# An RWKV layer with a routed feed-forward: the first block's keys and values by seven products, the recurrence's differences clipped by Relu on ScalarE

## The chip, the cores and the metric

The kernel runs on one core of one Trainium2 chip. The core has five engines that run side by side, each in the order of its own queue: TensorE (matrix products; the profile has PE for the products and PEld for its weight loads), VectorE (DVE), ScalarE (ACT), GpSimd (POOL) and SyncE (SP), which here only issues transfers. The metric is device microseconds for one execution of the whole program, a median over runs.

## The reference, cut to what matters

```python
xn = layernorm(x)                                  # x: 1 x 2048 x 512
r, v, k = split(einsum('btc,dc->btd', xn, W_rvk))  # three 512 x 512 weights

def step(carry, kv):                               # over the 2048 tokens, per channel
    p, q, o = carry
    kt, vt = kv
    no = maximum(o, u + kt)
    A, Bc = exp(o - no), exp(u + kt - no)
    y = (A * p + Bc * vt) / (A * q + Bc)
    no2 = maximum(w + o, kt)
    A2, B2 = exp(w + o - no2), exp(kt - no2)
    return (A2 * p + B2 * vt, A2 * q + B2, no2), y

attn = einsum('btc,dc->btd', sigmoid(r) * wkv(k, v), W_out)
# feed-forward: softmax over 12 choices, the best 2 taken; 8 are experts (512 -> 256 -> 512,
# silu(gate) * up, then down), 4 pass xn through
out = x + attn + ffn(xn)
```

## The kernel before

**Tiling.** The 2048 tokens are taken as four blocks of 512 (`b`), the 512 channels as four columns of 128 partitions (`c`). `xnT[b]` holds a block of normalised tokens, transposed. `wrvk_sb[0]`, `[1]` and `[2]` are the weights of r, v and k.

**Products of a block.** k and v of one column together are, plainly, eight matrix products of half a block by half the channels. They can be had from seven, with sums of tokens (`S1` to `S4`, `sum_tokens`) and of weights (`T2` to `T4`, `sum_weights`; the first is made in place by `sum_first_weights`, L413). Each product is two matmuls of 256 tokens. `sevens(b, c, with_r)` gives the seven as steps `m1` to `m7`, `pair(b, c)` strings them together for two columns and their r (`A`, `B`, `R`). Product 5 multiplies `S1` by the weights that `sum_first_weights` makes. After products 2 and 3 an addition on VectorE is owed (`owe`): k gets the second product straight from PSUM, v gets `more`.

**Block 0** is different in the kernel before: k of columns 0 and 1 is multiplied plainly in halves by `half_k`, v and r of these two plainly by `project`, and columns 2 and 3 by `seven`, which makes k and v by seven products and r plainly.

**Order.** Everything up to the end of the planned part stands in an order written by hand (`manual_schedule`): each engine runs its instructions as the program lists them. `products` is a generator of steps, each of 0.86 us of TensorE, and `fill(n)` lists the next n steps. The head does, in this order: norms and transposes of the four blocks with one or two steps between them (7 steps), `sum_weights` and the four token sums of block 0, the routing's first part on VectorE, `fill(9)`, a small product `pc`, more routing with `sum_first_weights()` at L816, `fill(16)`, the products `pi` in two halves with `fill(2)` between them, then `which_i`, `emit(2)` (lists two owed additions), and the copy of `pi` and what follows from it (L955 to L968). Then the gathers and first fetches are issued, and L1280 to L1289 list the last steps of the head among owed additions, token sums of block 1 and sums of r's weights (`sum_r_weights`).

**PSUM.** All eight banks are taken: `ps_o`, `ps_mm`, `ps_gu` and `ps_tr` have two each. Behind the last step of block 0 `change_banks` (L91) closes the last three and opens `gu` (1), `p2` (1), `p1` (2), `p3` (1) and `pr` (1) in their place; in the order of opening, `gu` and `p2` take the banks of `ps_mm`, `p1` those of `ps_gu`, and `p3` and `pr` those of `ps_tr`. A pool that takes the banks of another may be written once every tile of the old pool has been read for the last time, wherever in the order that read is listed.

**The planned part.** From L1292 a table of due times orders the rest: 16 units of the recurrence (`scan(b, c)`, each in five stages), 23 tiles of the experts (`first_half`, `second_half`), the products of blocks 1 to 3, and the output products (`attention`). `UNIT` sets the distance of two units. In a unit VectorE makes the running maximum o2 (L351), a2 (L353) and b2 (L354); ScalarE takes their exponentials (L356, L357); VectorE runs two more scans (L363, L365), copies the state (L372, L373), forms numerator and denominator (L374 to L376) and divides (L380, L382).

**Loads.** SP issues x of block 0, the weight of k, the classifier, x of blocks 1 and 2, the weight of v, x of block 3, the weight of r (L124 to L132).

Of the kernel before, what the change touches and what calls it, by code (L numbers as in the profile page):

```python
# [26 lines left out]
F32 = mybir.dt.float32  # L27
# [8 lines left out]
P = 128  # L36
# [27 lines left out]
def layer(ctx: ExitStack, tc: tile.TileContext, x, w_rvk, w_out, decay, first, cls, ebias, gu, down, out):  # L64
# [60 lines left out]
    load_w(2)  # L125
# [3 lines left out]
    load_x(2)  # L129
    load_w(1)  # L130
    load_x(3)
    load_w(0)  # L132
# [132 lines left out]
    first_k = {}  # L265

    def half_k(c, h):
        if h == 0:
            first_k[c] = ps_mm.tile([P, TB], F32, tag="mm", name=f"pk0_{c}")
        hs = slice(h * HALF, (h + 1) * HALF)  # L270
        for k in range(CC):
            nc.tensor.matmul(
                first_k[c][:, hs],
                wrvk_sb[2][:, k, c * P : (c + 1) * P],
                xnT[0][:, k, hs],
                start=(k == 0),
                stop=(k == CC - 1),
                skip_group_check=True,
            )
        if h == 1:  # L280
            kvr[0, c, "k"] = kvp.tile([P, TB], F32, tag="k", name=f"k0_{c}")
            nc.scalar.copy(kvr[0, c, "k"], first_k[c])
# [30 lines left out]
    def project(b, c, parts=(("k", 2), ("v", 1), ("r", 0))):  # L313

        n = f"{b}_{c}"
        for name, m in parts:
            ps = ps_mm.tile([P, TB], F32, tag="mm", name=f"p{name}{n}")
            for k in range(CC):
                nc.tensor.matmul(  # L319
                    ps,  # L320
                    wrvk_sb[m][:, k, c * P : (c + 1) * P],
                    xnT[b][:, k, :],
                    start=(k == 0),
                    stop=(k == CC - 1),
                )
                if k < CC - 1:
                    yield
            t = (erp if name == "r" else kvp).tile([P, TB], F32, tag=name, name=f"{name}{n}")
            if name == "r":
                nc.scalar.activation(t, ps, AF.Exp, scale=-1.0)  # L330
            else:
                nc.scalar.copy(t, ps)
            kvr[b, c, name] = t
            yield

    def scan(b, c):
# [9 lines left out]
        obv = wk1.tile([P, 3, TB + 1], F32, tag="obv", name=f"obv{n}")  # L346
        nc.vector.tensor_copy(obv[:, :, 0:1], s[:, 0:3].unsqueeze(2))
        o, bs, bvs = (obv[:, m, 0:TB] for m in range(3))
        o2, b2, bv = (obv[:, m, 1 : TB + 1] for m in range(3))
# [3 lines left out]
        nc.vector.scalar_tensor_tensor(a2, o, w, o2, ALU.add, ALU.subtract)  # L353
        nc.vector.tensor_sub(b2, k, o2)  # L354
        yield
        nc.scalar.activation(a2, a2, AF.Exp)  # L356
        nc.scalar.activation(b2, b2, AF.Exp)  # L357
# [3 lines left out]
        sums = wk1.tile([P, 2, TB], F32, tag="sums", name=f"sums{n}")  # L361
        sq, sp = sums[:, 0, :], sums[:, 1, :]
        nc.vector.tensor_tensor_scan(sq, bs, a2, s[:, 3:4], ALU.add, ALU.mult)  # L363
        nc.vector.tensor_mul(bv, b2, v)
# [3 lines left out]
        if b > 0:  # L368
            nc.scalar.activation(er, er, AF.Exp, scale=-1.0)
        num = yT[b][:, c, :]  # L370
        if b + 1 < NTB:
            nc.vector.tensor_copy(s[:, 0:3].unsqueeze(2), obv[:, :, TB : TB + 1])  # L372
            nc.vector.tensor_copy(s[:, 3:5].unsqueeze(2), sums[:, :, TB - 1 : TB])  # L373
        nc.vector.scalar_tensor_tensor(sq, b2, cf, sq, ALU.mult, ALU.add)  # L374
        nc.vector.scalar_tensor_tensor(er, er, 1.0, sq, ALU.add, ALU.mult)
# [48 lines left out]
    def sum_r_weights(first):  # L424
        if first:
            for n in (2, 3, 4):
                rsum[n] = sump.tile([P, 2, 2, P], F32, tag=f"R{n}", name=f"R{n}")
# [48 lines left out]
    def seven(b, c):  # L476

        n = f"{b}_{c}"
        cs = slice(c * P, (c + 1) * P)

        def bank(pool_, tag, name):
            return pool_.tile([P, TB], F32, tag=tag, name=f"{name}{n}")

        def place(pool_, name):
            kvr[b, c, name] = pool_.tile([P, TB], F32, tag=name, name=f"{name}{n}")
            return kvr[b, c, name]

        def multiply(ps, m, begin, end):
            a, w = factors(b, m)
            for k in range(2):  # L490
                nc.tensor.matmul(  # L491
                    ps[:, :HALF],
                    w[:, k, cs],
                    a[:, k, :],
                    start=(begin and k == 0),
                    stop=(end and k == 1),
                    skip_group_check=True,
                )

        def add(dst, src):  # L500
            nc.vector.tensor_add(dst, dst, src)

        def r_step(k):
            nc.tensor.matmul(  # L504
                pr, wrvk_sb[0][:, k, cs], xnT[b][:, k, :], start=(k == 0), stop=(k == CC - 1)
            )

        def next_sums(ns):
            if c == CC - 1 and b + 1 < NTB:
                for m in ns:  # L510
                    owe(lambda m=m: sum_tokens(b + 1, m))

        p1 = bank(ps_mm, "mm", "p1_")
        multiply(p1, 1, True, False)
        k = place(kvp, "k")
        nc.scalar.copy(k[:, :HALF], p1[:, :HALF])
        yield
        emit_owed()
        pr = bank(ps_tr, "tr", "pr")
        r_step(0)  # L520
        yield
        r_step(1)
        yield
        multiply(p1, 6, False, False)
        v = place(kvp, "v")
        nc.scalar.copy(v[:, :HALF], p1[:, :HALF])
        yield
        p3 = bank(ps_mm, "mm", "p3_")
        multiply(p3, 5, True, False)
        more = five.tile([P, TB], F32, tag="more", name=f"more{n}")  # L530
        nc.scalar.copy(more[:, HALF:], p3[:, :HALF])
        yield
        p2 = bank(ps_gu, "gu", "p2_")
        multiply(p2, 2, True, True)
        owe(lambda: add(k[:, :HALF], p2[:, :HALF]))
        next_sums((1, 2))
        yield
        multiply(p1, 7, False, False)
        nc.scalar.copy(v[:, HALF:], p1[:, :HALF])
        next_sums((3,))  # L540
        yield
        r_step(2)
        emit_owed()
        yield
        r_step(3)
        r = place(erp, "r")
        nc.scalar.activation(r, pr, AF.Exp, scale=-1.0)
        yield
        multiply(p1, 4, False, True)
        nc.scalar.copy(k[:, HALF:], p1[:, :HALF])  # L550
        yield
        multiply(p3, 3, False, True)
        nc.scalar.copy(more[:, :HALF], p3[:, :HALF])
        owe(lambda: add(v, more))
# [3 lines left out]
    def sevens(b, c, with_r):  # L560
# [8 lines left out]
        def at(m):  # L569
# [8 lines left out]
            if m in (1, 2, 5):  # L578
                ps[which] = bank(which, f"{which}{'r' if with_r else ''}_{n}")
# [22 lines left out]
        def next_sums(*ns):  # L602
            if c == CC - 1 and b + 1 < NTB:
                for m in ns:
                    owe(lambda m=m: sum_tokens(b + 1, m))
# [11 lines left out]
        def m5():  # L617
            src = multiply(5)
            t["more"] = five.tile([P, TB], F32, tag="more", name=f"more{'r' if with_r else ''}{n}")
            nc.scalar.copy(t["more"][:, HALF:], src)  # L620
# [18 lines left out]
        return {1: m1, 2: m2, 3: m3, 4: m4, 5: m5, 6: m6, 7: m7}, next_sums  # L639

# [20 lines left out]
    def owe(work):  # L661
        owed.append((clock[0] + 2, work))
# [7 lines left out]
    LEAD = 2  # L670
# [623 lines left out]
    STEPS = 2 * 2 * CC + 11 * (CC - LEAD) + 21 * (len(units) - CC) // 2  # L1294
# [116 lines left out]
```

## Time and profile before

| | |
|---|---|
| median of 3 runs | 362.3 us (361.89 to 362.86) |
| the profiled execution's own time | 362.48 us |
| its span, first to last instruction | 360.7 us |
| TensorE busy | 98% of the span |
| VectorE busy | 85% |
| ScalarE busy | 44% |
| VectorE in units of the recurrence, longest group (reciprocal, L380) | 53.7 us |
| chain that ended last | PE 73%, DVE 17%, DMA 5% |

The times lie 1.8 us above the span. A busy TensorE is not a TensorE at its peak, since the ends of matmuls are modelled: whether it is dense is read from the starts of its rows. A matmul in fp32 is recorded as two instructions, so a step of two 256-token matmuls is "x4". In a timeline a row gives the start, the duration, the engine, the line and the operation, the tiles written and read, and in brackets the idle time before it.

### The profile page before, as it was taken

To read this page: it belongs to the slowest core of one execution; us is meant where nothing else is said; L and a number is where in the kernel's file an instruction comes from. 1 tells how busy PE (TensorE), PEld (TensorE's weight loads), DVE (VectorE), ACT (ScalarE), POOL (GpSimd) and SP (SyncE) were. 2 spreads that over 40 slices of the span, in tenths; PEclk is the share of its full clock that TensorE was granted. 3 is DMA by queue.
4 is the path that set the end of the run, shared out by engine and by line. 5 is a ranking of instruction groups with operands and counts; after the bars stand their busy time and mean duration, and the time that the engine had idled before them with its cause. 6 is when DMAs were issued, how large, how long until landed. Compare 5 with 4: busy or idle time off the path is not lost.

```text
span 360.7 us, 5328 instructions
## 1 busy us (share of the span) xinstructions
PE 354.0 (98%) x1850; PEld 256.7 (71%) x1850; DVE 306.8 (85%) x531; ACT 159.0 (44%) x308; POOL 90.3 (25%) x118
## 2 busy tenths in 40 slices
PE   8999999999999999999999999999999999999996
PEld 3764578799865877547877688988776988854344
DVE  5879889959999997899695799997989589979971
ACT  3576222354643645525545454546453546432000
POOL 6000300431312232321321433323322124221130
PEclk9999999999999999999999999999999999999999
DMA  8999950795869699967999968979979986924782
GB/s 282 398 356 363 331 174 2 245 323 135 254 196 248 147 367 301 276 215 189 281 281 334 294 189 216 309 147 306 284 226 262 236 173 167 337 55 58 177 139 95
DMA packets 47132, 84.46 MB, mean 234 GB/s; under 512 B 26496, under 2 KB 26880, under 8 KB 43328
## 3 DMA queue, kind: packets, MB, share of 16 engines
q1 hardware_dynamic: 39792, 64.05, 56.2%
q0 software_dynamic: 7312, 20.06, 25.1%
q8 instruction: 15, 0.25, 0.3%
q14 instruction: 13, 0.11, 0.1%
HBM read 63.25 MB, written 19.27 MB: 229 GB/s over the span
## 4 chain that ended last, share of the span: by engine, by line
PE 73%; DVE 17%; DMA 5%; ACT 2%; issue 1%; SPq 0%; DVEq 0%; ACTq 0%
PE pg L1109 19%; PE p L592 17%; PE po L1057 8%; PE pr L592 7%; PE pw L1244 7%; DVE r L380 4%; PE p L491 3%; DMA x<-in_x_dram 3%; DMA wrvk<-in_w_rvk_dram 2%; PE pr L504 2%; PE pr L319 2%; DVE sums L365 2%; DVE sums L363 2%; PE p2r L592 1%; PE po L1061 1%
## 5 line engine op out<-in xcount | busy, mean ns | idle before, releaser
L1109 PEld LDWEIGHTS pg<-xgT,gw 128*128 128x128 f32 x672 | 78.1, 192 | 3.7 <-ACT xgT L1090 1.6
L1109 PE MATMUL pg<-xgT,gw 128*128 128x128 f32 x672 | 79.1, 275 | 0.2 <-ACT xgT L1090 0.2
L1145 POOL DMA_INDIRECT out_dram<-yo,to_i x23 | 40.4, 1758 | 142.9 <-ACT yo L1141 28.7
L1244 PE MATMUL pw<-wout_sb,yT 128*128 128x512 f32 x120 | 54.1, 593 | 0.7 <-DVE xrows L1256 0.6
L380 DVE RECIPROCAL r<-r 128x256 f32<-128x256 f32 x32 | 53.7, 1719 | 0.0
L1244 PEld LDWEIGHTS pw<-wout_sb,yT 128*128 128x128 f32 x120 | 22.3, 190 | 25.5 <-issue 24.8
L1057 PE MATMUL po<-dw,act 128*128 128x512 f32 x84 | 39.5, 592 | 0.0
L1015 POOL DMA_INDIRECT xg<-xs,token_i x23 | 26.4, 1148 | 44.6 <-DVE empty L963 25.2
L1121 ACT ACTIVATE act<-pg 128x256 f32<-128x256 f32 x23 | 8.8, 384 | 65.0 <-PE pg L1109 60.4
L1122 DVE SCALAR_TENSOR_TENSOR act<-act,pg 128x256 f32<-128x256 f32 x23 | 9.6, 417 | 21.0 <-ACT act L1121 21.0
L1090 ACT COPY xgT<-xq 128x1024 uint16<-128x1024 uint16 x22 | 25.6, 1161 | 2.6 <-DMA xq<-xp 2.6
L1057 PEld LDWEIGHTS po<-dw,act 128*128 128x128 f32 x84 | 16.0, 190 | 13.7 <-issue 12.7
L592 PE MATMUL p<-xnT,wrvk 128*128 128x256 f32 x96 | 24.7, 380 | 0.7 <-DVE k L624 0.7
L592 PE MATMUL p<-S,wrvk 128*128 128x256 f32 x96 | 24.7, 380 | 0.0
L592 PE MATMUL p<-S,T 128*128 128x256 f32 x96 | 24.6, 379 | 0.0
L363 DVE TENSOR_TENSOR_SCAN sums<-obv,state,a 128x512 f32<-128x512 f32 x16 | 20.5, 1280 | 4.1 <-ACT obv L357 4.0
L1082 ACT COPY xp<-xg 128x1024 uint16<-128x1024 uint16 x22 | 23.0, 1047 | 0.0
L592 PEld LDWEIGHTS p<-xnT,wrvk 128*128 128x128 f32 x96 | 18.0, 190 | 6.0 <-issue 2.6
L592 PEld LDWEIGHTS p<-S,T 128*128 128x128 f32 x96 | 18.2, 190 | 5.0 <-issue 2.9
L365 DVE TENSOR_TENSOR_SCAN sums<-obv,state,a 128x512 f32<-128x512 f32 x16 | 20.6, 1288 | 0.6
L592 PEld LDWEIGHTS p<-S,wrvk 128*128 128x128 f32 x96 | 17.9, 190 | 4.3 <-issue 1.4
L351 DVE TENSOR_TENSOR_SCAN obv<-wdec,state,k 128x512 f32<-128x512 f32 x16 | 20.4, 1277 | 0.0
(262 smaller groups left out, 576.1 us busy)
## 6 DMA issues: line engine op xcount, KB each, us to landing
gw<-in_gu_dram SPq DMA_DIRECT2D x25, 1024.0 KB, 7.4
dw<-in_down_dram SPq DMA_DIRECT2D x25, 512.0 KB, 4.9
x<-in_x_dram SPq DMA_DIRECT2D x16, 256.0 KB, 6.4
xs<-x SPq DMA_DIRECT2D x16, 256.0 KB, 4.6
wrvk<-in_w_rvk_dram SPq DMA_DIRECT2D x3, 1024.0 KB, 7.2
xrow<-xs SPq DMA_DIRECT2D x8, 256.0 KB, 7.3
out_dram<-xrow POOLq DMA_DIRECT2D x8, 256.0 KB, 8.2
xrows<-xs SPq DMA_DIRECT2D x8, 256.0 KB, 6.4
```

The costliest lines, as they stand in the source:

```text
L351: nc.vector.tensor_tensor_scan(o2, w.to_broadcast([P, TB]), k, s[:, 0:1], ALU.add, ALU.max)
L363: nc.vector.tensor_tensor_scan(sq, bs, a2, s[:, 3:4], ALU.add, ALU.mult)
L365: nc.vector.tensor_tensor_scan(sp, bvs, a2, s[:, 4:5], ALU.add, ALU.mult)
L380: nc.vector.reciprocal(er[:, hs], er[:, hs])
L592: nc.tensor.matmul(dst, rows_(k), a[:, k, :], start=(first and k == 0), stop=(k == 1), skip_group_check=True,)
L1015: nc.gpsimd.indirect_dma_start(out=xg, out_offset=None, in_=xs, in_offset=bass.IndirectOffsetOnAxis(ap=token[:, column(i) : column(i) + 1] ...
L1057: nc.tensor.matmul(out_, lhs[:, c, :], rhs[0][:, c, :], start=(c == 0), stop=(c == last))
L1082: nc.scalar.copy(xp, st[i]["xg"].bitcast(U16).rearrange("p (c h) -> p h c", h=2))
L1090: nc.scalar.copy(xgT.bitcast(U16).rearrange("p c (t h) -> p c t h", h=2), st[i]["xq"].rearrange("p (h c) t -> p c t h", h=2),)
L1109: nc.tensor.matmul(pg[:, c // IC, c % IC * P : (c % IC + 1) * P], w[0][:, k, rs], xgT[:, k, :], start=(k == 0), stop=(k == CC - 1),)
L1145: nc.gpsimd.indirect_dma_start(out=out, out_offset=bass.IndirectOffsetOnAxis(ap=index, axis=0), in_=yo[ps], in_offset=None, compute_op=ALU ...
L1244: nc.tensor.matmul(po, yT[b][:, c, j * P : (j + 1) * P], wout_sb[:, c, :], start=(c == 0), stop=(c == CC - 1),)
```

## The change

In block 0, `half_k` becomes `half_r`: r of columns 0 and 1 is multiplied plainly in halves, and r of columns 2 and 3 plainly by `project_r`. k and v of all four columns come from the seven products, as steps of a new generator `first_pair`, for columns 0 and 1 and then for 2 and 3, each with an order written out. `seven` and `project` go. r of block 0 is now copied from PSUM, and its exponential is taken in the unit, as in the other blocks. The weights are loaded in the order r, k, v: r's in the place of k's, the other two behind all of x. The head lists one step fewer before the token sums and one more behind them, and the sums and owed additions in another order.

In a unit, VectorE forms only d = o + w - k; ScalarE makes relu(d) and relu(-d) and takes the exponentials of their negatives. The two sums are kept in the same tile as o2, b2 and bv, the denominator goes to `a2`, and the state is copied by one instruction of ScalarE. `UNIT` goes from 16.75 to 16.5, and four places of `after` move by one.

```diff
     load_x(0)
-    load_w(2)
+    load_w(0)
...
     load_x(1)
     load_x(2)
+    load_x(3)
+    load_w(2)
     load_w(1)
-    load_x(3)
-    load_w(0)
...
-        nc.vector.scalar_tensor_tensor(a2, o, w, o2, ALU.add, ALU.subtract)
-        nc.vector.tensor_sub(b2, k, o2)
+        nc.vector.scalar_tensor_tensor(a2, o, w, k, ALU.add, ALU.subtract)
         yield
-        nc.scalar.activation(a2, a2, AF.Exp)
-        nc.scalar.activation(b2, b2, AF.Exp)
+
+        nc.scalar.activation(b2, a2, AF.Relu)
+        nc.scalar.activation(a2, a2, AF.Relu, scale=-1.0)
+        nc.scalar.activation(b2, b2, AF.Exp, scale=-1.0)
+        nc.scalar.activation(a2, a2, AF.Exp, scale=-1.0)
         yield
...
+        nc.vector.tensor_mul(bv, b2, v)
         nc.vector.tensor_tensor_scan(sq, bs, a2, s[:, 3:4], ALU.add, ALU.mult)
-        nc.vector.tensor_mul(bv, b2, v)
         nc.vector.tensor_tensor_scan(sp, bvs, a2, s[:, 4:5], ALU.add, ALU.mult)
...
-        if b > 0:
-            nc.scalar.activation(er, er, AF.Exp, scale=-1.0)
+        nc.scalar.activation(er, er, AF.Exp, scale=-1.0)
         num = yT[b][:, c, :]
-        if b + 1 < NTB:
-            nc.vector.tensor_copy(s[:, 0:3].unsqueeze(2), obv[:, :, TB : TB + 1])
-            nc.vector.tensor_copy(s[:, 3:5].unsqueeze(2), sums[:, :, TB - 1 : TB])
...
+        if b + 1 < NTB:
+            nc.scalar.copy(s.unsqueeze(2), obv[:, :, TB : TB + 1])
...
+    def first_pair(c, order):
+        A, _ = sevens(0, c, False)
+        B, _ = sevens(0, c + 1, False)
+        for name in order.split():
+            {"A": A, "B": B}[name[0]][int(name[1])]()
+            yield
...
     def all_products():
-        for name, m in (("v", 1), ("r", 0)):
-            for u in range(LEAD):
-                yield from project(*units[u], ((name, m),))
-        for u in range(LEAD, CC):
-            yield from seven(*units[u])
+        for c in (2, 3):
+            yield from project_r(0, c)
+        yield from first_pair(0, "A1 B1 A2 A6 B6 B2 A7 B7 A5 B5 A4 B4 A3 B3")
+        yield from first_pair(2, "A1 B1 A5 A6 B6 B5 A7 B7 A3 A4 B4 B3 A2 B2")
         change_banks()
...
-    fill(4)
-    emit(3)
+    fill(3)
+    sum_tokens(1, 1)
+    emit(1)
+    sum_tokens(1, 2)
+    emit(1)
     sum_r_weights(True)
-    emit(1)
-    emit(1, 1)
+    sum_tokens(1, 3)
+    emit(2)
+    sum_tokens(1, 4)
     sum_r_weights(False)
-    emit(1)
+    emit(2)
     mixed_tiles()
     head = False
-    fill(8)
+    fill(9)
...
-    UNIT = 16.75
-    after = {10: (0, 0), 12: (0, 1), 16: (0, 2), 18: (0, 3), 27: (1, 0), 29: (1, 1), 36: (1, 2), 37: (1, 3)}
+    UNIT = 16.5
+    after = {10: (0, 0), 12: (0, 1), 16: (0, 2), 18: (0, 3), 26: (1, 0), 28: (1, 1), 35: (1, 2), 36: (1, 3)}
```

More of the change, by code (lines that the diff above doesn't have):

```diff
@@ L262, in turn_block, with half_r @@
             nc.scalar.copy(xnT[b][:, c, cols], pt[:, cols])
-    first_k = {}
-    def half_k(c, h):
+    first_r = {}
+    def half_r(c, h):
         if h == 0:
-            first_k[c] = ps_mm.tile([P, TB], F32, tag="mm", name=f"pk0_{c}")
+            first_r[c] = ps_mm.tile([P, TB], F32, tag="mm", name=f"pr0_{c}")
         hs = slice(h * HALF, (h + 1) * HALF)
@@ L272, in half_k @@
             nc.tensor.matmul(
-                first_k[c][:, hs],
-                wrvk_sb[2][:, k, c * P : (c + 1) * P],
+                first_r[c][:, hs],
+                wrvk_sb[0][:, k, c * P : (c + 1) * P],
                 xnT[0][:, k, hs],
@@ L280, in half_k @@
         if h == 1:
-            kvr[0, c, "k"] = kvp.tile([P, TB], F32, tag="k", name=f"k0_{c}")
-            nc.scalar.copy(kvr[0, c, "k"], first_k[c])
+            kvr[0, c, "r"] = erp.tile([P, TB], F32, tag="r", name=f"r0_{c}")
+            nc.scalar.copy(kvr[0, c, "r"], first_r[c])
     lgs = {}
@@ L311, in layer, with project_r @@
     yT, kvr = {}, {}
-    def project(b, c, parts=(("k", 2), ("v", 1), ("r", 0))):
+    def project_r(b, c):
         n = f"{b}_{c}"
[L316 to L334, printed above, removed]
+        ps = ps_mm.tile([P, TB], F32, tag="mm", name=f"pr{n}")
+        for k in range(CC):
+            nc.tensor.matmul(
+                ps,
+                wrvk_sb[0][:, k, c * P : (c + 1) * P],
+                xnT[b][:, k, :],
+                start=(k == 0),
+                stop=(k == CC - 1),
+            )
+            if k < CC - 1:
+                yield
+        kvr[b, c, "r"] = erp.tile([P, TB], F32, tag="r", name=f"r{n}")
+        nc.scalar.copy(kvr[b, c, "r"], ps)
+        yield
     def scan(b, c):
@@ L343, in scan @@
             yT[b] = xyp.tile([P, CC, TB], F32, tag="xy", name=f"yT{b}")
-        obv = wk1.tile([P, 3, TB + 1], F32, tag="obv", name=f"obv{n}")
-        nc.vector.tensor_copy(obv[:, :, 0:1], s[:, 0:3].unsqueeze(2))
+        obv = wk1.tile([P, 5, TB + 1], F32, tag="obv", name=f"obv{n}")
+        nc.vector.tensor_copy(obv[:, :, 0:1], s.unsqueeze(2))
         o, bs, bvs = (obv[:, m, 0:TB] for m in range(3))
-        o2, b2, bv = (obv[:, m, 1 : TB + 1] for m in range(3))
+        o2, b2, bv, sq, sp = (obv[:, m, 1 : TB + 1] for m in range(5))
@@ L358, in scan @@
+        nc.scalar.activation(a2, a2, AF.Relu, scale=-1.0)
+        nc.scalar.activation(b2, b2, AF.Exp, scale=-1.0)
+        nc.scalar.activation(a2, a2, AF.Exp, scale=-1.0)
         yield
         v = kvr[b, c, "v"]
-        sums = wk1.tile([P, 2, TB], F32, tag="sums", name=f"sums{n}")
-        sq, sp = sums[:, 0, :], sums[:, 1, :]
+        nc.vector.tensor_mul(bv, b2, v)
         nc.vector.tensor_tensor_scan(sq, bs, a2, s[:, 3:4], ALU.add, ALU.mult)
-        nc.vector.tensor_mul(bv, b2, v)
         nc.vector.tensor_tensor_scan(sp, bvs, a2, s[:, 4:5], ALU.add, ALU.mult)
@@ L367, in scan @@
         er = kvr[b, c, "r"]
-        if b > 0:
-            nc.scalar.activation(er, er, AF.Exp, scale=-1.0)
+        nc.scalar.activation(er, er, AF.Exp, scale=-1.0)
         num = yT[b][:, c, :]
-        if b + 1 < NTB:
-            nc.vector.tensor_copy(s[:, 0:3].unsqueeze(2), obv[:, :, TB : TB + 1])
-            nc.vector.tensor_copy(s[:, 3:5].unsqueeze(2), sums[:, :, TB - 1 : TB])
-        nc.vector.scalar_tensor_tensor(sq, b2, cf, sq, ALU.mult, ALU.add)
-        nc.vector.scalar_tensor_tensor(er, er, 1.0, sq, ALU.add, ALU.mult)
+        nc.vector.scalar_tensor_tensor(a2, b2, cf, sq, ALU.mult, ALU.add)
@@ L376, in scan @@
+        nc.vector.scalar_tensor_tensor(er, er, 1.0, a2, ALU.add, ALU.mult)
         nc.vector.scalar_tensor_tensor(num, bv, cf, sp, ALU.mult, ALU.add)
         yield
+        if b + 1 < NTB:
+            nc.scalar.copy(s.unsqueeze(2), obv[:, :, TB : TB + 1])
         def divide(h):
@@ L424, in sum_r_weights, with new @@
     def sum_r_weights(first):
+        def new(n):
+            t = sump.tile([P, TB], F32, tag=f"R{n}", name=f"R{n}")
+            rsum[n] = t.rearrange("p (k q n) -> p k q n", k=2, q=2)
         if first:
-            for n in (2, 3, 4):
-                rsum[n] = sump.tile([P, 2, 2, P], F32, tag=f"R{n}", name=f"R{n}")
+            new(3)
             rsum[1] = r_weights(0, 1)
@@ L431, in sum_r_weights @@
         else:
+            new(2)
+            new(4)
             nc.vector.tensor_add(rsum[2], rsum[3], r_weights(0, 0))
@@ L474, in r_factors @@
         return factors(b, n)[0], w
[L476 to L556, printed above, removed]
@@ L577, in at @@
                 return ps["pr"][:, h * HALF : (h + 1) * HALF]
-            if m in (1, 2, 5):
+            if m in (1, 2, 5) and not banks:
+                pool_, tag = {"p1": (ps_mm, "mm"), "p2": (ps_gu, "gu"), "p3": (ps_tr, "tr")}[which]
+                ps[which] = pool_.tile([P, TB], F32, tag=tag, name=f"{which}_{n}")
+            elif m in (1, 2, 5):
                 ps[which] = bank(which, f"{which}{'r' if with_r else ''}_{n}")
@@ L602, in next_sums @@
         def next_sums(*ns):
-            if c == CC - 1 and b + 1 < NTB:
+            if c == CC - 1 and 0 < b < NTB - 1:
                 for m in ns:
@@ L618, in m5 @@
             src = multiply(5)
-            t["more"] = five.tile([P, TB], F32, tag="more", name=f"more{'r' if with_r else ''}{n}")
+            if (b, c) in ((0, 2), (0, 3)):
+                t["more"] = sump.tile([P, TB], F32, tag=f"R{2 * c - 2}", name=f"more{n}")
+            else:
+                t["more"] = five.tile([P, TB], F32, tag="more", name=f"more{'r' if with_r else ''}{n}")
             nc.scalar.copy(t["more"][:, HALF:], src)
@@ L639, in sevens @@
         return {1: m1, 2: m2, 3: m3, 4: m4, 5: m5, 6: m6, 7: m7}, next_sums
+    def first_pair(c, order):
[3 more added lines that the diff above has]
+            {"A": A, "B": B}[name[0]][int(name[1])]()
+            yield
     def pair(b, c):
@@ L669, in layer @@
     units = [(b, c) for b in range(NTB) for c in range(CC)]
-    LEAD = 2
     def whole(gen):
@@ L709, in layer @@
     norm(0, late_js)
-    half_k(0, 0)
-    half_k(1, 0)
+    half_r(0, 0)
+    half_r(1, 0)
     turn_block(0, late_js)
@@ L720, in layer @@
         if b == 0:
-            half_k(0, 1)
+            half_r(0, 1)
         else:
@@ L725, in layer @@
         if b == 0:
-            half_k(1, 1)
+            half_r(1, 1)
         fill(1)
@@ L1293, in layer @@
     DONE = 7 + 9 + 16 + 2 + 12
-    STEPS = 2 * 2 * CC + 11 * (CC - LEAD) + 21 * (len(units) - CC) // 2
-    UNIT = 16.75
-    after = {10: (0, 0), 12: (0, 1), 16: (0, 2), 18: (0, 3), 27: (1, 0), 29: (1, 1), 36: (1, 2), 37: (1, 3)}
+    STEPS = 2 * CC + 7 * CC + 21 * (len(units) - CC) // 2
+    UNIT = 16.5
+    after = {10: (0, 0), 12: (0, 1), 16: (0, 2), 18: (0, 3), 26: (1, 0), 28: (1, 1), 35: (1, 2), 36: (1, 3)}
     groups = -(-(STEPS - DONE) // CC) + len(after)
```

## The prediction

> **What bounds the kernel now.** I read the busy shares first, then who TensorE waited for, then the starts of its rows.
>
> ```profile
> PE 354.0 (98%) x1850; PEld 256.7 (71%) x1850; DVE 306.8 (85%) x531; ACT 159.0 (44%) x308; POOL 90.3 (25%) x118
> PE warm L703 <- DVE ones L148: 1.1, 1, 1.1
> PE p L592 <- DVE k L624: 0.7, 1, 0.7
> PE pw L1244 <- DVE xrows L1256: 0.6, 1, 0.6
> PE pt L261 <- ACT x L247: 0.3, 1, 0.3
> PE pg L1109 <- ACT xgT L1090: 0.2, 1, 0.2
> ```
>
> From its first matmul on TensorE waits for another engine only 1.8 us in all (0.7 + 0.6 + 0.3 + 0.2). A busy share alone would not prove that it sets the pace, so I went through its timeline: from 8 us to 356 us a step of two matmuls starts 0.86 us after the one before and a tile's 16 up-products take 3.57 us, everywhere. Also behind 318 us, where the chain of waits runs through VectorE, the output products stand back to back from 324.0 to 340.5 (38 records in 16.5 us). So there is hardly a hole in which lost TensorE time could be won back: a wait of TensorE is worth its length, and so is a step less. The stage that decides is the head, where the change lists products and VectorE work in another order:
>
> ```profile
> 37.03 7.03 PE L319 MATMUL pr<-xnT,wrvk 128*128 128x512 f32 x16
> 43.90 0.22 PE L781 MATMUL pc<-hotb,ones 128*128 128x136 bf16 x1
> ...
> 44.58 1.08 PE L491 MATMUL p<-xnT,wrvk 128*128 128x256 f32 x4
> 45.49 1.88 PE L504 MATMUL pr<-xnT,wrvk 128*128 128x512 f32 x4
> 47.20 1.03 PE L491 MATMUL p<-S,T 128*128 128x256 f32 x4
> 48.07 1.03 PE L491 MATMUL p<-S,wrvk 128*128 128x256 f32 x4
> ...
> 61.59 1.59 PE L933 MATMUL pi<-tok,lowhot 128*128 128x200 bf16 x16
> ```
>
> ```profile
> 46.61 1.22 DVE L416 TENSOR_TENSOR wrvk<-wrvk,wrvk 128x1024 f32<-128x1024 f32 x1
> ...
> 64.29 0.36 DVE L955 COPY pis<-pi 128x200 f32<-128x200 f32 x1
> ...
> 65.76 0.41 DVE L501 TENSOR_TENSOR k<-k,p 128x256 f32<-128x256 f32 x1
> 66.09 0.68 DVE L445 TENSOR_TENSOR S<-xnT 128x512 f32<-128x512 f32 x1
> ...
> 71.28 0.68 DVE L501 TENSOR_TENSOR v<-v,more 128x512 f32<-128x512 f32 x1
> ```
>
> The first fence is TensorE's order, the second VectorE's at the same time. Product 5 (`p<-S,wrvk`) starts at 48.07, right behind L416, which makes its weights and ends at 47.83: between `pc` and it stand four steps that do not need them. And the k addition at 65.76 is VectorE's first work behind the copies of `pi`, ahead of the sums.
>
> **The products: -1.7 us.** Before, block 0 has 38 steps behind `half_k` (16 of `project`, 22 of `seven`), after it 36 (8 and 28), and `half_r` is as long as `half_k`. Two steps at 0.86 us (from 47.20 to 48.07 is one) are 1.7 us.
>
> **First wait: +3.3 us.** The head lists 7, 9, 16 and 2 steps as before. After the change the first 8 are r and the next 8, up to `pc`, are A1 B1 A2 A6 B6 B2 A7 B7 of the first pair. Step 17, the first behind `pc`, is A5, product 5. TensorE reaches it at 44.58, and nothing in the change moves `sum_first_weights`: L416 still ends at 47.83. Queued behind A5 is all of TensorE. It starts near 47.9, 3.3 us late. Both halves of `pi` are late next, and with them L955 on VectorE.
>
> **Second wait: +8.2 us.** The first three of the last steps are A2 and B2 of the second pair and then, as step 37, A1 of block 1. Between them `change_banks` puts `p1` on the banks of `ps_gu`, where A2 and B2 have just left their products. These are read by the owed additions to k of columns 2 and 3, and the owed list runs k, k, v, v, v, v, k, k: `emit(2)` behind the tiles takes the first two, and the last two stand at the very end of the new order. So A1 waits for VectorE's whole sequence. Call TensorE's end of `pi` zero. VectorE needs 0.2 to see it, 1.47 from L955 to the first work behind it (64.29 to 65.76), and then, from start to start in the rows of 65.76 to 71.88 (0.60 to 0.61 for 512 columns, 0.72 where the next one needs the result, 0.33 for a k addition): ten at about 0.60, two at 0.72, 0.33 and 0.41, together 8.2. The additions end at 9.9. TensorE is at A1 after A2 and B2, at 1.7: it waits 8.2 us. Next late is `turn(0)`, at 73.39 before, by both waits. The gathers and fetches (to landing 6.8 and 7.4 us) are issued off VectorE's copies, before these sums, and get 8 us more to land, so they add nothing.
>
> **The clock: +2.6 us.** No row of the head shows TensorE after such a pause. Nearest are two: after the 0.7 us wait at 101.85 the next steps come at the full rate, so the lower end is 0. At the start, after idling, the warm-up's loads come slowly first:
>
> ```profile
> 6.16 0.15 PEld L703 LDWEIGHTS <-ones 128*128 128x128 bf16 x1 [0.28 <-issue]
> 6.50 1.18 PEld L703 LDWEIGHTS <-ones 128*128 128x128 bf16 x6 [0.18 <-issue]
> ```
>
> From 1.06 to about 6.4 us they stand 0.43 apart, one to a row, then 0.21 (six in 1.18): half the rate for 5.3 us, which is 2.6 us lost, although the granted clock reads 1.00 in all of it. A pause of 8.2 us is nearer to the start's than to 0.7 us, so I take 2.6 for it, nothing for the one of 3.3, and 5.3 (both) for the upper end.
>
> [...]
>
> **The recurrence: +0.3 us.** VectorE loses L354 (0.60 us from start to start, 16 times) and the two state copies (0.32, 12 times): 13.4 us, against four more additions in block 0 (1.9 us). It is not the bound, so this buys at most the waits of TensorE for it, 0.7 at 101.85 and 0.6 at 342.5. ScalarE gains 32 relus, 12 copies and 4 exponentials. Relu is in no row: it can't cost less than nothing, and the nearest rows, L356 and L357, have 0.63 and 0.62 us (0.53 to 0.60 from start to start); I take 0.60. The copy is nearest to L947 with 0.2 us. Together 24 us on an engine with 202 us idle. What it delays are the operations queued behind the four in a row, 1.2 us each time. Where an `xgT` copy (L1090) follows soon and TensorE waits for it, that shows: at 161.55, where 0.2 us are lost already, and at 300.98, where 1.0 is spare. That is 1.2 + 0.2. At the other units 1.0 to 4.7 us are spare. VectorE's scans wait for the exponentials 4.0 us in all; the next one then has 1.2 us less lead and 0.6 less work before it, some 0.6 us in each of five units. The last unit's product stands 0.6 us later for it, about as much as TensorE waits there now. With 1.4 lost and 1.1 of the old waits won, I take +0.3, with -1.5 and +3 as ends.
>
> [...]
>
> **Loads: 0.** The last of the three weights has landed by 21.4 us (issued at 13.26, 8.1 us in the chain), and VectorE first adds weights at 29.9. These 8.5 us hide the new order; all of them are queued on SP within the same 13.6 us, with nothing new behind. If the cover were gone, VectorE would stall at L409.
>
> **The sum.** 362.5 (profiled execution) - 1.7 + 3.3 + 8.2 + 2.6 + 0.3 = 375.2. That execution lies 0.2 above the median, so **375.0 us**.
>
> **Rivals.**
> - *The banks do not hold A1.* If `p1` came to lie elsewhere, or the additions were earlier, the second wait and the clock go: 375.0 - 8.2 - 2.6 = 364.2. For it: no row before shows such a wait. Against: eight banks are full, and before the k addition is listed first. 8 in 100.
> - *Product 5 is not late*, since the change does not do what its order says and L416 comes earlier. Then L955 starts at 64.0, VectorE-bound, A1 is ready at 64.75 (63.02, the end of `pi`, and two steps) and waits for 73.7: 362.3 - 1.7 + 8.9 + 2.6 + 0.3 = 372.4. Against: L816 is not touched. 5 in 100.
> - *VectorE has set the pace all along*, and TensorE makes up what it loses. For it: 17% of the chain and nines in VectorE's slices. Then 13.4 - 1.9 = 11.5 us less work would cover the two waits' 11.5 us, the two steps and the two waits on VectorE go, 362.3 - 1.7 - 1.3 = 359.3. It decides from the point where TensorE has over 11.5 us of holes behind 76 us. Its rows have under 2. 5 in 100.
> - *More is lost behind ScalarE's queue* than I saw, or both waits go cold: 378 to 381. 6 in 100.
>
> **How the numbers follow.** The first forecast has 76 in 100. With both ends of the clock (0, 5.3) and the recurrence (-1.5, +3) it runs from 370.6 to 380.4; both at their ends together is unlikely, so I keep **370.5 to 378.5**, which also holds the second rival, about 8 in 10. A kernel like this can be told from no change beyond 0.3%, 1.1 us. Faster has the third rival and a little of the first, 0.06; the same 0.02; slower 0.92.
>
> **What would show it.** Right: TensorE idle some 3.3 us at 44.6, before the first product on `S` and `wrvk`, waiting for the VectorE operation of L416; idle some 8 us before the first product of block 1, waiting for an addition to k; weight loads at double spacing behind that; the middle dense, shifted by 10 to 13 us. Wrong: A1 following B2 at once, or holes in TensorE's middle that shrink by as much as the head loses.

## The result, and the profile after

| | before | after |
|---|---|---|
| median | 362.35 us (6 runs, 361.89 to 364.14) | 378.24 us (6 runs, 375.75 to 381.22) |
| ratio to before, 95% interval | | 1.043 (1.038 to 1.049) |
| profiled execution's own time, its span | 362.48, 360.7 us | 378.54, 376.8 us |
| granted TensorE clock, mean of the span | 1.000 | 0.982 |

The change makes the kernel 15.9 us slower. The forecast was 375.0 us, with 370.5 to 378.5 as its range: the median lies 0.3 us inside its upper end, and three of the six runs lie above it.

The page of the kernel after, its row of busy shares and its row of granted clocks over 40 slices (9 is full):

```profile
PE 357.8 (95%) x1874; PEld 264.1 (70%) x1874; DVE 296.6 (79%) x495; ACT 181.6 (48%) x364; POOL 89.9 (24%) x118
PEclk9999989859999999999999999999999999999999
```

Who TensorE waited for, in the same kernel (total us, times, longest):

```profile
PE p L512 <- DVE k L547: 8.1, 1, 8.1
PE p L512 <- DVE wrvk L410: 2.8, 1, 2.8
...
PE pw L1172 <- DVE xrows L1184: 1.0, 1, 1.0
...
PE pg L1037 <- ACT xgT L1018: 0.8, 2, 0.4
```

Busy time rose on TensorE though it has two steps fewer, mainly since matmuls on a halved clock last longer (one of 256 columns 0.63 us for 0.38). VectorE fell from 85 to 79%: its load was lightened, and the kernel is slower. The two forecast waits stand on top of the list: for `sum_first_weights` (L410 here), and for the additions to k (L547). TensorE's timeline around them:

```profile
45.18 0.22 PE L720 MATMUL pc<-hotb,before 128*128 128x136 bf16 x1
48.24 2.81 PE L512 MATMUL p<-S,wrvk 128*128 128x256 f32 x8 [2.84 <-DVE wrvk L410]
50.84 2.81 PE L512 MATMUL p<-xnT,T 128*128 128x256 f32 x8
53.49 1.89 PE L512 MATMUL p<-S,wrvk 128*128 128x256 f32 x8
...
68.44 1.91 PE L512 MATMUL p<-xnT,wrvk 128*128 128x256 f32 x8
78.41 2.08 PE L512 MATMUL p<-xnT,wrvk 128*128 128x256 f32 x4 [8.05 <-DVE k L547]
...
83.56 1.03 PE L512 MATMUL p<-S,T 128*128 128x256 f32 x4
```

And VectorE's:

```profile
46.97 1.22 DVE L410 TENSOR_TENSOR wrvk<-wrvk,wrvk 128x1024 f32<-128x1024 f32 x1
...
68.64 0.37 DVE L883 COPY pis<-pi 128x200 f32<-128x200 f32 x1 [4.16 <-PE pi L861]
...
70.13 0.69 DVE L444 TENSOR_TENSOR S<-xnT 128x512 f32<-128x512 f32 x1
...
77.61 0.74 DVE L547 TENSOR_TENSOR k<-k,p 128x256 f32<-128x256 f32 x2
```

Product 5 could start at 45.24 (0.06 us behind the last matmul of `pc`, as its rows follow one another) and starts at 48.24: 3.0 us. A2 and B2 of the second pair are over at 70.17 (68.44 and two steps of 0.86), and A1 of block 1 starts at 78.41: 8.24 us. Behind each pause the starts lie too far apart: four steps take 5.25 us (48.24 to 53.49) for 3.45, three take 5.15 (78.41 to 83.56) for 2.59. The granted clock in windows of 1 us of the same kernel shows why. The columns are the window, its length, busy time of PE, PEld, DVE, ACT and POOL (with instructions), the granted clock, DMA share and GB/s:

```profile
48.00:49.00 1.00, 0.76 (x4) 0.68 (x5) 0.85 (x6) 0.00 (x0) 0.00 (x0) 1.00 2.41 786
49.00:50.00 1.00, 1.00 (x5) 0.80 (x4) 0.80 (x5) 0.37 (x1) 0.00 (x0) 0.64 0.20 66
...
52.00:53.00 1.00, 1.00 (x4) 0.80 (x4) 0.90 (x5) 0.21 (x1) 0.00 (x0) 0.66 0.25 98
...
73.00:74.00 1.00, 0.00 (x0) 0.00 (x0) 0.97 (x3) 0.00 (x0) 1.00 (x1) 0.58 0.76 225
...
83.00:84.00 1.00, 1.00 (x6) 0.83 (x5) 0.00 (x0) 0.24 (x1) 0.00 (x0) 0.80 0.00 0
```

In the windows left out the clock is 0.50 up to 52 and from 74 to 83, and 1.00 from 53 to 73. A window at 0.64 was at half rate for 0.72 of its microsecond, so the clock falls at 49.28 and comes back at 52.68; by the same reading it is at half from 73.16 to 83.40.

So the 16.1 us between the spans (376.8 - 360.7) are: `pc` reached 0.66 later (44.56 for 43.90), first wait 3.0, slow steps 1.8, second wait 8.24, slow steps 2.56, two steps less -1.73, and 1.6 behind 84 us. The experiments are about which of these is caused by what.

### The profile page after: what moved, and what is told of

Same layout as the page of the kernel before. It is cut to its first block, busy times and chain, and to the rows that moved or that the text cites. A ratio compares the mean times of both kernels' runs of the same rounds, so it can differ in the third digit from the quotient of the medians.

```text
span 376.8 us, 5373 instructions
## 1 busy us (share of the span) xinstructions
PE 357.8 (95%) x1874; PEld 264.1 (70%) x1874; DVE 296.6 (79%) x495; ACT 181.6 (48%) x364; POOL 89.9 (24%) x118
## 4 chain that ended last, share of the span: by engine, by line
PE 71%; DVE 14%; DMA 6%; ACT 5%; SPq 2%; issue 1%; DVEq 0%; ACTq 0%
PE p L512 22%; PE pg L1037 19%; PE pw L1172 8%; PE po L985 7%; PE pr L512 7%; DMA gw<-in_gu_dram 2%; DMA wrvk<-in_w_rvk_dram 2%; PE pg L989 2%; DMA x<-in_x_dram 2%; DVE r L374 2%; SPq L115 1%; PE p2r L512 1%; PE po L989 1%; DVE obv L359 1%; DVE obv L360 1%
## 5 line engine op out<-in xcount | busy, mean ns | idle before, releaser
L512 PE MATMUL p<-xnT,wrvk 128*128 128x256 f32 x128 | 33.7, 391 | 8.1 <-DVE k L547 8.1
L512 PE MATMUL p<-S,wrvk 128*128 128x256 f32 x128 | 34.3, 395 | 2.8 <-DVE wrvk L410 2.8
L512 PEld LDWEIGHTS p<-xnT,wrvk 128*128 128x128 f32 x128 | 24.1, 194 | 15.2 <-DVE k L547 8.5
L512 PE MATMUL p<-S,T 128*128 128x256 f32 x128 | 32.4, 381 | 0.2 <-ACT v L535 0.2
L512 PEld LDWEIGHTS p<-S,wrvk 128*128 128x128 f32 x128 | 25.0, 198 | 6.9 <-DVE wrvk L410 3.0
L512 PEld LDWEIGHTS p<-S,T 128*128 128x128 f32 x128 | 23.9, 191 | 5.3 <-issue 1.0
L358 DVE TENSOR_TENSOR obv<-obv,v 128x512 f32<-128x512 f32 x16 | 11.0, 690 | 12.4 <-ACT obv L353 12.4
L1069 ACT ACTIVATE yo<-po,wplace 128x512 f32<-128x512 f32 x23 | 15.9, 690 | 10.0 <-PE po L985 9.9
```

What stands on the lines that cost most here:

```text
L512: nc.tensor.matmul(dst, rows_(k), a[:, k, :], start=(first and k == 0), stop=(k == 1), skip_group_check=True,)
L1069: nc.scalar.activation(yo, po, AF.Identity, scale=weight[:, column(i) : column(i) + 1])
```

## The experiments

The kernel before stood beside each one on the same chip, at medians of 362.5 to 362.7 us. Ratios are to it, with 95% intervals.

**The two additions to k ahead of the sums.**

```diff
-    fill(3)
+    fill(2)
+    emit(2, 4)
+    fill(1)
     sum_tokens(1, 1)
...
     sum_r_weights(False)
-    emit(2)
     mixed_tiles()
```

> Only the place of the two additions to k of columns 2 and 3 is changed: they come ahead of the token sums of block 1. Theory (the bank of block 1's first product is held by these two additions): B2's product ends at 70.2, VectorE sees it 0.2 later and needs 0.74 for both, so the first product of block 1 starts near 71.1 and waits 0.9 us, not 8.24; the slow steps behind it (5.15 us for three that take 2.59) go too. 378.2 - 7.3 - 2.6 = 368.3 us. Rival (VectorE's whole sequence of sums sets the pace there, and the wait only moves to the next steps that need S and R): no more than 2 or 3 us are won, 375 us or more, and the trace shows TensorE waiting for sums of tokens or of r's weights instead.

Measured 368.03 us, 1.013 (1.009 to 1.016). TensorE's timeline of this kernel:

```profile
69.08 1.91 PE L512 MATMUL p<-xnT,wrvk 128*128 128x256 f32 x8
71.57 1.13 PE L512 MATMUL p<-xnT,wrvk 128*128 128x256 f32 x4 [0.58 <-DVE k L547]
72.54 1.03 PE L512 MATMUL p<-S,wrvk 128*128 128x256 f32 x4
```

A1 now starts 0.76 us behind B2's end (69.08 + 1.73), and the steps behind it are 0.86 to 0.97 apart. Some 10 us of the loss came from the place of two additions that take 0.74 us together. VectorE's sums come as late as before (the last ends at 78.99) and hold nothing up for long: the first rival is out.

**The weight sum early.**

```diff
     nc.vector.tensor_add(hotb[:, :NT, :], hot[:, 0, :, :E], hot[:, 1, :, :E])
+    sum_first_weights()
     fill(9)
...
-    sum_first_weights()
     up_i = narrow8("up_i", I32)
```

> Only the place of the weight sum for product 5 is changed: it is VectorE's first work behind hotb, not behind vals. Theory: it ends at 45.1, before pc does (45.24), so product 5 follows at once: 3.0 us of wait and 1.8 us of slow steps behind it go (four steps took 5.25 us, not 3.45). The end of pi comes 4.8 us earlier, VectorE's copy of pi 4.2 (it has own work up to 64.5), so the second wait grows by 0.6: 378.2 - 4.8 + 0.6 = 374.0 us. Rival (the four steps are slow for another reason than the pause, such as a clock that falls by itself or the work beside them): only the wait goes, 378.2 - 3.0 = 375.2 us, and the four steps still take 5.2 us. Second rival (routing on VectorE is what counts and is now 1.2 us later): 378 or more.

Measured 373.04 us, 1.030 (1.026 to 1.033). Product 5 starts at 45.02, 0.06 behind the last row of `pc`, and no step up to the second pause is slow. The second wait grows to 8.5 us (8.05 in the kernel after), about as expected. The three steps behind it take 4.74 us there, 2.15 too long, where they took 2.56 too long in the kernel after.

**Both.**

> The two moves together. Theory (two waits with a slow clock behind each make the whole loss, and the recurrence about none): end of pi at 63.8, the two additions to k end at 66.7, block 1's first product is reached at 65.5 and waits 1.2 us: 378.2 - 4.8 - 7.0 - 2.6 = 363.8 us, within 2 us of the kernel before, since the two steps fewer (-1.7) stand against the rest of the trace (+1.6) and a wait of 1.2. Rival (ScalarE's longer queue or the seven products themselves cost it): 367 us or more, with TensorE's waits for ScalarE grown. Rival on the other side (the recurrence pays once the waits are gone): 361 us or less.

Measured 364.41 us, 1.0042 (1.0018 to 1.0066). With both moves the granted clock is 1.00 in every slice. The two waits and what follows them were 13.8 of the 15.9 us. The kernel is still no faster than before: the rival that the recurrence pays once the waits are gone is out.

**TensorE kept busy in the pauses.** This kernel adds products of ones that nothing reads.

```diff
+    def keep_warm(n):
+        for _ in range(n):
+            nc.tensor.matmul(
+                pc_bank[:, HALF:],
+                ones,
+                ones.unsqueeze(1).to_broadcast([P, HALF // P, P]),
...
     nc.tensor.matmul(pc, before, hotb, start=False, stop=True)
+    keep_warm(25)
...
-    fill(3)
+    fill(2)
+    keep_warm(68)
+    fill(1)
```

> Products of ones that nothing reads are added in the two pauses of the changed kernel: 25 of 256 columns in bf16 behind pc (some 2.7 us at the full rate) and 68 behind B2 (some 7.3 us); the waits stay as long as they are. Theory (the steps behind both pauses are slow because TensorE was idle): the four steps behind the first take 3.45 us and the three behind the second 2.59, 378.2 - 1.8 - 2.6 = 373.8 us. Rival (they are slow because of the waits' releasers, of transfers or of VectorE beside them): the steps stay slow, 378 us. If only the long pause makes TensorE slow: 375.6 us.

Measured 374.21 us, 1.031 (1.027 to 1.035), 4.0 us below the kernel after. Its TensorE timeline:

```profile
45.16 2.89 PE L713 MATMUL pc<-ones 128*128 128x256 bf16 x25
48.17 1.99 PE L512 MATMUL p<-S,wrvk 128*128 128x256 f32 x8
50.00 1.89 PE L512 MATMUL p<-xnT,T 128*128 128x256 f32 x8
...
68.44 7.59 PE L713 MATMUL pc<-ones 128*128 128x256 bf16 x68
76.65 1.13 PE L512 MATMUL p<-xnT,wrvk 128*128 128x256 f32 x4 [0.63 <-DVE k L547]
```

The waits are as long as before, and two steps take 1.83 us at once (48.17 to 50.00) where they took 2.60. The granted clock stays at 1.00 here from 40 to 100 us, where the kernel after has 0.50 behind each pause: it is the idleness that makes TensorE slow there.

**The banks in another order.**

```diff
-        for name, n in (("gu", 1), ("p2", 1), ("p1", 2), ("p3", 1), ("pr", 1)):
+        for name, n in (("p1", 2), ("gu", 1), ("p2", 1), ("p3", 1), ("pr", 1)):
```

> The changed kernel with one edit: where the banks change hands, the pool of block 1's first products opens first, so that it takes the banks of ps_mm, and those of A2 and B2, which wait for the additions to k, go to the turning of tokens and to the second products. Theory (the wait is for the bank, not for a value): A1, A5, R1 and A6 follow B2 at once, and the fifth step of block 1, A2, waits until the additions end near 78.4. Four steps (3.45 us) come out of the pause: 378.2 - 3.4 = 374.8 us, with a wait of some 4.8 us ahead of A2, still followed by slow steps. Rival (A1 waits for a value or for VectorE's sums, whatever the bank): A1 still waits 8 us, 378.2 us.

Measured 373.98 us, 1.033 (1.028 to 1.038). TensorE's timeline:

```profile
66.52 2.77 PE L512 MATMUL p<-xnT,wrvk 128*128 128x256 f32 x12
69.13 1.03 PE L512 MATMUL p<-S,wrvk 128*128 128x256 f32 x4
69.99 1.03 PE L512 MATMUL pr<-xnT,wrvk 128*128 128x256 f32 x4
70.85 1.03 PE L512 MATMUL p<-S,T 128*128 128x256 f32 x4
76.47 1.52 PE L512 MATMUL p<-xnT,wrvk 128*128 128x256 f32 x4 [4.59 <-DVE k L547]
```

A1 is now the third step of the first row, and the wait has gone with the bank to A2, the fifth step of block 1, which has no operand in common with the additions. The wait is for the bank.

**The recurrence, alone and undone.** First the new recurrence in the kernel before, then the old one in the kernel after, then the old one with both moves (the edits are those of the change, one way or the other).

> The kernel before with the changed recurrence alone (the products, loads, order and distance of units stay). Theory (the recurrence is off the bound; it can win back no more than the 1.1 us that TensorE waits for VectorE now, and loses some where xgT's copies and the scans queue behind ScalarE's four operations): 0 to 1.5 us slower, 362.7 + 0.8 = 363.5 us. Rival (13.4 us less of VectorE's work pay): 361.5 us or less. Second rival (ScalarE's queue is what costs the changed kernel its unexplained rest and more): 365 us or more.

Measured 365.38 us, 1.0079 (1.0053 to 1.0105): 2.6 us slower, not 0.8. In this kernel TensorE waits 1.8 us for the last unit where it waited 0.6, and 1.5 us for `xgT` where it waited 0.2:

```profile
PE pw L1244 <- DVE xrows L1256: 1.8, 1, 1.8
PE pg L1109 <- ACT xgT L1090: 1.5, 2, 1.0
```

> The changed kernel with the recurrence of before; the exponential of r stays in the unit for all blocks. Theory: both waits and both slow stretches stay and the time moves by the recurrence alone, down 0 to 1.5 us: 377.4 us. Rival (the new recurrence is a large part of the loss): 374 us or less. Rival on the other side (it had saved time that the waits hide): 379.5 us or more.

Measured 374.59 us, 1.032 (1.029 to 1.035): 3.7 us below the median of the kernel after, whose own runs lie 5.5 us apart.

> Both moves (the weight sum and the two additions to k early) and the recurrence of before. Theory: 0 to 1.5 us below the kernel with both moves, 364.4 - 0.8 = 363.6 us. Rival (with the waits gone VectorE's load counts): 365.5 us or more.

Measured 362.05 us, 0.9975 (0.9958 to 0.9991), 2.4 us below the kernel with both moves and the new recurrence.

My size for the recurrence fell in all three. The traces show where it goes. The kernel after and the one with the old recurrence start the same up-products within 0.02 us of each other from 147.5 to 306.0. That is not because the middle costs nothing. Before that the kernel after is ahead: by 0.39 us at 92.63, from the head, and by 0.97 at 123.53 (the same products start at 124.50 in the other), mostly because TensorE waits 0.2 us for the copy of v in it and not 1.4. Then both wait for the weights of an expert. These are TensorE's weight loads and SP's issue of the fetch, first in the kernel after and then in the one with the old recurrence:

```profile
125.05 0.16 PEld L989 LDWEIGHTS pg<-gw,xgT 128*32 128x32 f32 x8 [1.37 <-DMA gw<-in_gu_dram]
115.76 0.34 SPq L964 DMA_DIRECT2D gw<-in_gu_dram  x1
...
125.06 0.14 PEld L990 LDWEIGHTS pg<-gw,xgT 128*32 128x32 f32 x5 [0.41 <-DMA gw<-in_gu_dram]
115.77 0.34 SPq L965 DMA_DIRECT2D gw<-in_gu_dram  x1
```

On SP a transfer of `xp` stands ahead of this fetch (at 113.10 in the kernel after), which ScalarE's copy releases at 113.07 in both kernels. ScalarE begins the unit's activations at 107.41 in the kernel after and at 108.37 in the other, and four operations instead of two use up this lead before the copies. So a lead of 1.0 us, most of it from the product that is listed ahead of the scans, and a loss of 1.0 us behind the relus cancel there. From 306.0 on, TensorE in the old recurrence's kernel:

```profile
316.52 3.73 PE L1038 MATMUL pg<-xgT,gw 128*128 128x128 f32 x32
...
339.16 28.88 PE L1173 MATMUL pw<-wout_sb,yT 128*128 128x512 f32 x66
```

and in the kernel after:

```profile
317.02 3.84 PE L1037 MATMUL pg<-xgT,gw 128*128 128x128 f32 x32 [0.35 <-ACT xgT L1018]
...
356.38 1.95 PE L1172 MATMUL pw<-wout_sb,yT 128*128 128x512 f32 x4
359.30 10.54 PE L1172 MATMUL pw<-wout_sb,yT 128*128 128x512 f32 x24 [0.96 <-DVE xrows L1184]
```

Twice something is late. The `xgT` copy of 317 stands behind four operations on ScalarE and not two, and the up-products start 0.5 us later, the next ones 0.6. And the output products, 66 in one row with the old recurrence, are broken at 358.1 to 359.30 (356.38 and two steps): they wait for VectorE's last unit. VectorE's timeline in the last unit, in the kernel with the old recurrence:

```profile
346.47 0.74 DVE L1185 SCALAR_TENSOR_TENSOR xrow<-xrow,zw,pw 128x512 f32<-128x512 f32 x1
347.31 1.28 DVE L358 TENSOR_TENSOR_SCAN sums<-obv,state,a 128x512 f32<-128x512 f32 x1
```

and in the kernel after, where the first operation that needs an exponential is the product of b2 and v (L358):

```profile
347.15 0.74 DVE L1184 SCALAR_TENSOR_TENSOR xrow<-xrow,zw,pw 128x512 f32<-128x512 f32 x1
349.17 0.69 DVE L358 TENSOR_TENSOR obv<-obv,v 128x512 f32<-128x512 f32 x1 [1.28 <-ACT obv L353]
```

There is no other work left to put between, so VectorE stands still for the exponentials, 0.76 us in the unit before and 1.28 in the last. From the copy of the state to the first operation behind its division the last unit takes 13.31 us for 12.72, 0.6 longer: 1.28 of waiting, less the 0.6 of the operation that VectorE no longer does. The one before takes 18.01 for 17.33, 0.7 longer, since there the dropped operation stood ahead of a wait for an expert's tile and saves nothing. That makes 0.6 for `xgT` and 1.3 for the two units, against 1.8 us between the two spans (376.8 - 375.0). A test of the place:

```diff
+        if (b, c) in units[-3:]:
+            nc.vector.scalar_tensor_tensor(a2, o, w, o2, ALU.add, ALU.subtract)
+            nc.vector.tensor_sub(b2, k, o2)
+            yield
+            nc.scalar.activation(a2, a2, AF.Exp)
+            nc.scalar.activation(b2, b2, AF.Exp)
+        else:
...
```

> Both moves and the new recurrence, but the differences of the last three of 16 units are formed on VectorE as before. Theory (the relus cost only where nothing covers them: 0.6 us ahead of the xgT copy near 316, and 0.6 to 0.7 in each of the last two units, where VectorE's chain sets TensorE's last wait): 364.3 - 1.9 = 362.4 us, without a wait of TensorE for the last unit. Rival (the cost of the recurrence is spread over all units, 0.15 us each): 363.9 us.

Measured 362.80 us, 1.0001 (0.998 to 1.002): 1.6 us for three units of 16, and TensorE's wait for the last unit is gone. So 1.6 of the 2.4 us lie at the end, where nothing covers the longer chain. The 0.7 us to the kernel with the old recurrence throughout stay open; the other 13 units still have the relus.

**R1 ahead of A1.**

```diff
+        first = "R1 A1 A5" if (b, c) == (1, 0) else "A1 A5 R1"
-        order = "A1 A5 R1 A6 A2 R5 A7 A3 R6 A4 B1 R2 B5 B6 R7 B3 B7 R3 B2 B4 R4".split()
+        order = (first + " A6 A2 R5 A7 A3 R6 A4 B1 R2 B5 B6 R7 B3 B7 R3 B2 B4 R4").split()
```

> Both moves, the new recurrence, and in block 1's first pair the step R1, which needs neither a bank of the second products nor a sum, goes ahead of A1. Theory (what is left of the second wait, 1.1 us, is the time that VectorE needs for the two additions behind pi, and any step that needs neither fills it): one step of 0.86 us fills it, 364.4 - 0.9 = 363.5 us, with a wait of 0.2 us left. Rival (R1's own bank is held as well, or the wait moves to the sum that A5 needs): 364.4 us.

Measured 364.26 us, 1.0034 (1.0012 to 1.0056), against 364.41 without it: nothing won, the rival is right. A1 waits 0.2 us for the addition, but A3, six steps on, now waits 0.4 for the fourth token sum, and the steps between are up to 0.1 late each; from A2 of the second pair to A4 of block 1 it is 10.96 us, as it was 10.95. Close behind `pi` VectorE's sums do set the pace, by about a microsecond.

**The order of loads.**

```diff
     load_x(2)
-    load_x(3)
     load_w(2)
+    load_x(3)
     load_w(1)
```

> Both moves and the recurrence of before, with the loads in before's pattern: r's weight, the classifier, x of blocks 1 and 2, k's weight, x of block 3, v's weight. In seven profiles with the new order of loads TensorE waits 0.2 to 1.7 us in its first products of r or ahead of them, in two with the old one it doesn't. Theory (that is jitter of the first loads, which the loads queued behind them do not change): 362.05 us, within 0.4. Rival (the new order of loads costs the head): 361.2 us, and no wait in the first products.

Measured 361.76 us, 0.9969 (0.9951 to 0.9988), against 362.05 without this edit, with TensorE waiting 1.3 us for r's weight. The order of the later loads is not the reason; why this first weight comes late in most profiles with r's weight first and in neither with k's is open. In the profile of the kernel after itself it was not late: of the 0.66 us at `pc`, 0.36 are there by 36 us, most of it behind the second tile of x, which VectorE could start on at 5.09 us and not at 4.36. The other 0.3 arise at 38.41, where a weight load waits 0.40 us for ScalarE's copy of r out of PSUM (L327), a wait that comes with the change and is in the best kernel too.

**The best of it.** Both moves, the old recurrence with the product of b2 and v ahead of the first scan, R1 first, and before's pattern of loads.

```diff
+        nc.vector.tensor_mul(bv, b2, v)
         nc.vector.tensor_tensor_scan(sq, bs, a2, s[:, 3:4], ALU.add, ALU.mult)
-        nc.vector.tensor_mul(bv, b2, v)
```

> Both moves, the recurrence of before with one change of order (b2 times v ahead of the scan of the denominator, so that the buffer of v comes free 1.2 us earlier), R1 ahead of A1, and the loads in before's pattern. Theory: TensorE's wait of 1.4 us for the copy of v goes but for 0.2, and the rest of the second wait (0.9 of 1.1): 362.05 - 1.2 - 0.5 = 360.3 us. Rival (TensorE's waits turn up elsewhere, since VectorE is as full as before): 362 us.

Measured 360.64 us, 0.994 (0.992 to 0.996): 0.6% faster than the kernel before. The wait for the copy of v in the kernel with both moves and the old recurrence, then all of TensorE's waits in this one but for the warm-up:

```profile
PE p L513 <- ACT v L536: 1.4, 1, 1.4
...
PE pr L272 <- DMA wrvk<-in_w_rvk_dram: 0.5, 1, 0.5
PE p L513 <- DVE S L451: 0.4, 1, 0.4
PE pt L261 <- ACT x L247: 0.3, 1, 0.3
PE p L513 <- DVE k L548: 0.2, 1, 0.2
PE p L513 <- ACT v L536: 0.2, 1, 0.2
```

The wait for the copy of v, 1.4 us with the old order of the scans, is 0.2. So one part of the changed recurrence is worth keeping, and it is not the one that the change was about: the product listed first, which frees a buffer. No run moves this product alone. The kernel with R1 first has the same order of products and scans, but the rest of the new recurrence and the change's loads: it took 364.26 us, 3.6 more, of which the loads were 0.3. So without the gain by the order the new recurrence costs an estimated 3.3 us (3.6 - 0.3).

## Why the prediction was right

- **What bounds the kernel.** Held. VectorE got 10.2 us less to do (306.8 to 296.6) and no run shows a gain by that.
- **The products, -1.7.** Not measured by itself, and the new `UNIT` and places of `after` were not varied alone. It fits: the best kernel's span is 1.9 us below before's (358.8 for 360.7); its waits behind the one for x (`pt`) come to 1.3 us and before's to 1.5 (0.7, 0.6 and 0.2), so some 1.7 are left for the two steps.
- **First wait, 3.3.** 3.0: right in place and cause. L410 ended 0.36 later than forecast and `pc` came 0.66 later.
- **Second wait, 8.2.** 8.24, in place, cause and size; that it is the bank is shown by the kernel with the banks in another order.
- **The clock, 2.6.** Mis-sized: 4.4 (1.8 and 2.56), and 4.0 by the kernel that was kept busy. The step that failed is "I take 2.6 for it, nothing for the one of 3.3": behind the shorter pause, 2.84 us of idle time, the clock was at half as well, for 3.40 us. That the long pause cost 2.56 us, close to the 2.6, is luck: the size was taken from another situation, the start, and in the kernel with the weight sum early such a pause cost 2.15. The sentence that a granted clock of 1.00 goes with half the rate at the start misled me as well: behind both pauses the granted clock is 0.50 and says just what the steps do.
- **The recurrence, 0.3.** Mis-sized: 1.8 in the spans, 2.4 to 2.6 in medians (with both moves, and in the kernel before). The step that failed is "The last unit's product stands 0.6 us later for it, about as much as TensorE waits there now". It treats a wait that exists as room; more lateness of the same releaser is added to it (0.6 became 1.8 in the kernel before with the new recurrence alone). And the delay counts twice, as the last two units follow each other on VectorE without a gap. The 1.2 us for `xgT` at 161.55 and 300.98 were 0.5 at 317 and 0.4 at 102 in the kernel after, and 0.5 at 85.59 and 1.0 at 162.77 in the kernel before with the new recurrence. What ScalarE's copies release further on was not in the sum: the fetch of weights at 115.76, 1.0 us, hidden by a lead of the same size.
- **Loads, 0.** No step waited for the two weights that come later. The head was still 0.66 us later, by the first x and by a copy of r that the sum did not have.
- **Rivals.** That more is lost behind ScalarE's queue or with both pauses cold, 378 to 381 at 6 in 100, is what came, next to the first forecast: each of its two parts happened in a smaller size. Both mis-sized terms were too small, so the forecast is 3.2 us low, and that the range held by 0.3 us is luck. The sum with the measured terms is 362.5 - 1.7 + 3.0 + 8.2 + 4.4 + 1.8 + 0.7 = 378.9, for 378.54 of the profiled execution.

## What to carry to other kernels

In an order written by hand, the last read of a bank is part of the next product's path (a wait of 8.24 us here): list the operations that give a bank back ahead of sums that nobody needs yet. A step moved forward needs its operands moved forward with it. Work shifted from a busy engine to an idle one is free only where other work stands between the two ends of the longer chain and where no copy that others wait for queues behind it, so the last units of a recurrence need looking at by themselves (three units of 16 held 1.6 of the 2.4 us here).

## What the runs showed of the hardware

**The same pause was followed by half the clock in three profiles and not in a fourth.** By the reading above, the clock of the kernel after turns at 49.28, 52.68, 73.16 and 83.40 us: it is at half for 3.40 us and, in and behind the longer pause, for 10.24. Read the same way, it is at half from 49.72 to 53.12 with the old recurrence, 3.40 us, and from 67.86 to 78.10 with the weight sum early, 10.24 us. The four turns of the kernel after are 3.40, 20.48 and 10.24 us apart, which is 1, 6 and 3 times 3.41 (34.12 / 10). Whether the clock turns in steps of a fixed length was not tested. Three profiles have the same first pause of 2.84 us and lose 1.8 us behind it (four steps take 5.25, 5.24 and 5.25 us for 3.45 in the kernels after, with the additions first, and with the old recurrence). The one with the banks in another order has this pause of 2.84 us too, but a granted clock of 1.00 from 43 to 58 us, and its four steps take 3.56 (48.00 to 51.56). Its second pause, of 4.59 us, ends at 76.47, and only then the clock falls:

```profile
77.00:78.00 1.00, 1.00 (x4) 0.82 (x3) 0.86 (x6) 0.00 (x0) 0.00 (x0) 0.54 0.98 401
...
80.00:81.00 1.00, 1.00 (x5) 0.86 (x4) 0.00 (x0) 0.11 (x1) 0.00 (x0) 0.75 0.00 0
```

so that it is at half from 77.08 to 80.50, 3.42 us. In the kernel after TensorE had been back at work for 1.04 us when the clock fell at 49.28 (from 48.24), with the old recurrence for 1.14 (48.58 to 49.72). What decides whether a pause of 2.84 us is followed by half the clock no run shows. The four runs of the kernel with the additions first differ as well: they have mean clocks of 0.993, 0.995, 0.995 and, the fastest, 1.000, though only the first was traced.

**The changed kernel scatters more, in part for this.** Its six runs have mean clocks of 0.977 to 0.990. A mean of 0.982 over 376.8 us is 13.6 us at half, as in its trace (3.40 and 10.24); by the same sum the runs at 0.990 were at half for an estimated 7.5 us and the one at 0.977 for 17.4. The two runs at 0.990 took 375.75 and 377.94 us, the two at 0.977 and 0.978 took 379.52 and 381.22. It is not all of the scatter: the kernel with both moves has its clock at 0.998 to 1.000 in all of its twelve runs, and they lie 3.3 us apart.
